# Attention output projection on float16 pairs, with Wo's rows pre-scaled on GpSimd and its squares taken in the down stage

## The chip, the cores and the metric

The kernel runs on one core of a Trainium2 chip. The metric is the device time of one execution in microseconds (us), smaller being better. A core has five engines that run their own instruction streams in order and wait for each other through semaphores: TensorE (PE for its matmuls, PEld for its weight loads), VectorE (DVE), ScalarE (ACT), GpSimd (POOL), and SyncE (SP), which here issues all DMAs from one queue.

## The reference

A layer norm of x (1024 x 512) feeds two branches, attention and a feed-forward branch with 4-bit weights. The result is x plus the attention output times a SiLU of the feed-forward output. Cut to what matters:

```python
xn = layernorm(x)
q, k = rmsnorm(xn @ Wq.T, q_norm_w), rmsnorm(xn @ Wk.T, k_norm_w)   # 32 query heads, 8 key heads
v = xn @ Wv.T                                                      # 8 value heads of 128
scores = q . k / sqrt(128) + alibi_slope * (key - query), causal
out = softmax(scores) @ v                                          # 32 heads of 128 -> 4096
s = out @ Wo.T                                                     # 4096 -> 512
g = silu(ffn(xn))                                                  # gate, up, down, group-dequantized
return x + s * g
```

## The kernel before, in words

The order of every engine's work is written out by hand. There are four stages.

**Gate and up, then down.** The two first feed-forward products run over 14 tiles of 128 hidden features. The down product then loops over the same 14 tiles (`it`, 0 to 13) and, in each, over two halves of the 1024 rows (`tb`). It works on float32r pairs: ACT copies a high part (`dnh`, `hh`, L102), DVE subtracts it to get the low part (`dnl`, `hl`, L104), and PE does three matmuls per product, high x high, high x low, low x high, in `mm3` (L108 to L110). The down weights are loaded as integers with their zeros and scales (`dn_load`, L409 to L414), dequantized by DVE (L419) and GpSimd (L420). The tiles with the tags `gs` and `us` hold gate and up sums and are free from about the fifth iteration on.

**Projections.** Twelve projections of 512 columns (four times keys and values of a pair of head groups, then two of queries) run over 8 row tiles each, on float16 pairs. `al`, the factor that scales each value column into float16's range, comes from the sums of squares of Wv; its reciprocal with the constants lands in `rv`, one factor per partition and group of heads (`undo`, L527).

**Attention.** 8 groups of heads, 4 query blocks of 256 rows each, 4 heads in a block: 128 units of 2 query tiles, so 256 steps. A block is 8 steps. In most groups the blocks come in the order 2, 3, 0, 1, and block 3 has the most keys, 896 and 1024. `step(n)` does, in this order, the scores of step n on PE, the exponentials of step n - 1 (DVE L816, ACT L817), the high half of the probabilities of n - 3 (ACT L827), the low half of n - 4 (DVE L836) with a DMA transpose of it on SP (L837), the product with the values of n - 9 on PE (`av`), and one group of three output-projection matmuls at n - 18. `pT` holds the transposed probabilities of four units. Scores have two PSUM buffers.

**Output projection.** When a unit's `av` is complete, ACT writes its high half `oh` times `rv` (L864) and DVE the low half `ol` (L870), both as float32r. Wo's 4096 x 512 rows come in 32 tiles of 128 x 512: `load_wo` (L775) on SP, `split_wo` with ACT's copy `woh` (L781) and GpSimd's subtraction `wol` (L782), both float32r. A tile's load comes 10 steps and its split 6 steps before the group's first use, four tiles at every second step, so that in the order above loads stand in steps 8 to 14 and splits in steps 12 to 18 of a group's 32 (block 3 is steps 8 to 15). The products of a group's four heads add up in PSUM (`op`); `accumulate` adds them on DVE to `y` (L905 copy for the first group, L907 add) and, for the last group, multiplies them by the gate (L910).

```python
        for lead, act in ((WO_SPLIT, split_wo), (WO_LOAD, load_wo)):
            w, r = divmod(m + lead, NB * BS)
            if 0 <= w < HKV and r in range(0, 2 * NH, 2):
                act(w, r // 2)
```

Of the kernel before, what the change touches and what calls it, by code (L numbers as in the profile page):

```python
# [10 lines left out]
F32 = mybir.dt.float32  # L11
F32R = mybir.dt.float32r
# [9 lines left out]
P = 128  # L22
# [30 lines left out]
VALUES_BLOCK = 3  # L53

WO_SPLIT = 6
WO_LOAD = 10

GATE_LOADS = [25, 26, 28, 30]
# [12 lines left out]
def attention_gated_by_ffn_kernel(ctx, tc, x, gu_w, gu_z, gu_s, dn_w, dn_z, dn_s, wq, wkv, wo, qnw, knw, out):  # L71
# [43 lines left out]
    ones_bf = const.tile([P, P], BF16, name="ones_bf")  # L115
    ve.memset(ones_bf, 1.0)
    rv = const.tile([P, HKV], F32, name="rv")
    wn = const.tile([P, HD], F32, name="wn")
    cs = const.tile([P, NH], F32, name="cs")
    rc = const.tile([P, 1], F32, name="rc")  # L120
# [309 lines left out]
    def dn_split_h(it, tb):  # L430
# [2 lines left out]
        split_r(h[:, it, tb * 512 : tb * 512 + 512], hh, hl)  # L433
        dn_h_hl[it, tb] = (hh, hl)


    qwb = wp.tile([P, HD], F32, name="qwb")
    kwb = wp.tile([P, HD], F32, name="kwb")
# [28 lines left out]
    class Projection:  # L467
# [55 lines left out]
        def undo(self):  # L523

            if self.kind == "kv":
                ve.reciprocal(self.ri, self.ri)
                ve.tensor_scalar(rv[:, 2 * self.i : 2 * self.i + 2], self.ri, 1.0 / (X_SCALE * P_SCALE), None, ALU.mult)  # L527

        def split_head(self, i):
            if i == 0:  # L530
# [157 lines left out]
    for it in range(NI):  # L688
        for tb in range(2):
            if it == 0:  # L690
                two = [pair(f"dn_ps{tb}_{i}") for i in range(2)]
                acc[tb] = [two[i // 2][:, i % 2, :] for i in range(4)]
            if tb == 0:
                if it + 2 < NI:
                    dn_dequant(it + 2)
                if it + 3 < NI:
                    dn_load(it + 3)
                if it + 1 < NI:
                    dn_split_w(it + 1)
            if it + 1 < NI:  # L700
                dn_split_h(it + 1, tb)
            wh, wl = dn_w_hl[it]
            hh, hl = dn_h_hl.pop((it, tb))
            for i in range(4):
                c = slice(i * P, i * P + P)
                mm3(acc[tb][i], (hh[:, c], hl[:, c]), (wh, wl), it == 0, it == NI - 1)
            if tb:
                if it in (1, 2):
                    gu_total((NI - 1, None), it - 1)
                elif it == 3:  # L710
                    gu_finish(0)
                elif it == 4:
                    gu_finish(1)
                elif it == 5:
                    norm_weights()
                elif NI - 6 <= it < NI - 1:
                    prepare(0, 8 - NI + it)
                if it == NI - 2:
                    prepare(1, -1)
            if it == NI - 1:  # L720
                for i in range(4):
                    go = h[:, i, tb * 512 : tb * 512 + 512]
                    se.activation(go, acc[tb][i], AF.Silu)
                    sp.dma_start(gd[tb * 4 + i], go)
# [42 lines left out]
    def load_queries(g, qb):  # L767
# [2 lines left out]
            qT[g, qb].rearrange("p t a g q -> p t (a g q)"), qd[g][qb * NQT : (qb + 1) * NQT].rearrange("t p c -> p t c")  # L770
        )

    def load_wo(g, i):
        wor[g, i] = late[0].tile([P, DM], F32, tag="wor", name=f"wor{g}_{i}", bufs=2)
        sp.dma_start(wor[g, i], wo[(g * NH + i) * HD : (g * NH + i + 1) * HD, :])  # L775

    def split_wo(g, i):
        woh[g, i] = late[0].tile([P, DM], F32R, tag="woh", name=f"woh{g}_{i}", bufs=5)
        wol[g, i] = late[0].tile([P, DM], F32R, tag="wol", name=f"wol{g}_{i}", bufs=5)
        raw = wor.pop((g, i))  # L780
        se.copy(woh[g, i], raw)  # L781
        ge.tensor_tensor(wol[g, i], raw, woh[g, i].bitcast(F32), ALU.subtract)  # L782

    def relative(g):

        rel = trel[g] = ap1.tile([P, S], F32, tag="trel", name=f"trel{g}")
        if g == 0:
            ge.iota(rel, pattern=[[-1, S]], base=S - P, channel_multiplier=1, allow_small_or_imprecise_dtypes=True)
            ge.affine_select(rel, rel, pattern=[[-1, S]], compare_op=ALU.is_ge, fill=1e20, base=S - P, channel_multiplier=1)
            ge.tensor_scalar(rel, rel, rc, float(SLOPES[NH - 1]), ALU.mult, ALU.mult)  # L790
        else:
            ge.tensor_scalar(rel, trel[g - 1], float(SLOPES[g * NH + NH - 1] / SLOPES[g * NH - 1]), None, ALU.mult)
# [65 lines left out]
            )  # L858

    def heads_hi(u):  # L860
        oh = late[0].tile([P, QB], F32R, tag="oh", name=f"oh{u}", bufs=8)
        ol = late[0].tile([P, QB], F32R, tag="ol", name=f"ol{u}", bufs=8)
        g = units[u][0]
        se.activation(oh, av_ps[u], AF.Copy, scale=rv[:, g : g + 1])  # L864
        oT[u] = (oh, ol)

    def heads_lo(u):
        oh, ol = oT[u]
        g = units[u][0]
        ve.scalar_tensor_tensor(ol, av_ps.pop(u), rv[:, g : g + 1], oh.bitcast(F32), ALU.mult, ALU.subtract)  # L870

    nb = len(units) // NH

# [25 lines left out]
    def accumulate(b, i):  # L899
        g, qb = blocks[b]  # L900
        ps = op_ps.pop((b, i))
        t = qb * NQT + i
        yt = y_[0][:, t, :]
        if g == 0:
            ve.tensor_copy(yt, ps)  # L905
        elif g < HKV - 1:
            ve.tensor_tensor(yt, yt, ps, ALU.add)  # L907
        else:
            gt = gates[b][:, 0, i]
            ve.tensor_tensor(gt, gt, ps, ALU.mult)  # L910
# [12 lines left out]
    def step(n):  # L923
        nonlocal last_ps
        if n < nn:
            u, qt = order[n]
            g, qb, hh = units[u]
            b = u // NH
            if qt == 0 and hh == 1 and b + 1 < nb:
                load_queries(*blocks[b + 1])  # L930
            if qt == 0 and hh == 3 and g + 1 < HKV:
                if b % NB == KEYS_BLOCK:
                    relative(g + 1)
                    load_keys(g + 1)
# [12 lines left out]
        b, r = divmod(n - AV_LAG - BS - 2, BS)  # L947
        if 0 <= b < nb - 1 and r % NH == NH - 1 and n < nn + AV_LAG + 1:
            accumulate(b, r // NH)
        finish_step()  # L950
        m = n - AV_LAG - BS - 1

        def project():
            b, r = divmod(m, BS)
            if 0 <= b < nb - 1:
                out_proj(b, *divmod(r, NH))

        if at(n - AV_LAG):
# [12 lines left out]
        b, r = divmod(n - AV_LAG, BS)  # L971
        if r == 2 and b in GATE_LOADS:
            gate_load(nb - NB + GATE_LOADS.index(b))
        if b in GATE_SUMS and 0 <= r - GATE_STEP < NQT:
            gate_partial(nb - NB + GATE_SUMS.index(b), r - GATE_STEP)
        for lead, act in ((WO_SPLIT, split_wo), (WO_LOAD, load_wo)):
            w, r = divmod(m + lead, NB * BS)
            if 0 <= w < HKV and r in range(0, 2 * NH, 2):
                act(w, r // 2)

    last_ps = None
    relative(0)
    early = 0
    for k, p in enumerate(projections):
        if k == len(projections) - 3:
            load_keys(0)
            load_values(0)
            load_queries(*blocks[0])
        for t in range(NT):
            prepare(k + 1, t)  # L990
            if t == NT - 2:
                prepare(k + 2, -1)
            if k + 2 < len(projections) and t < KT:
                projections[k + 2].load(t)
            if t == HT:
# [54 lines left out]
```

## Time and profile before

| | |
|---|---|
| median of 3 runs | 1081.96 us (1079.21 to 1083.37) |
| the profiled execution | 1087.19 us, span 1085.4 us, granted clock 0.987 |
| PE busy | 1025.6 us, 94% of the span |
| DVE busy | 885.4 us, 82% |
| ACT busy | 797.9 us, 74% |
| POOL busy | 362.7 us, 33% |
| DMA moved | 198.10 MB, mean 183 GB/s |
| stages, about | gate and up to 137 us, down to 217, projections to 500, attention to the end |

Busy time is the union of an engine's instructions; matmuls overlap, so their durations add up to more than it. "L108" is a line of the kernel. For a group of instructions the page gives busy us, the mean ns of one, then the engine's idle time before them and what ended it. The waits list who waited for whom, in all, how many times, and the longest.

### The profile page before, as it was taken

To read this page: it belongs to the slowest core of one execution; us is meant where nothing else is said; L and a number is where in the kernel's file an instruction comes from. 1 tells how busy PE (TensorE), PEld (TensorE's weight loads), DVE (VectorE), ACT (ScalarE), POOL (GpSimd) and SP (SyncE) were. 2 spreads that over 40 slices of the span, in tenths; PEclk is the share of its full clock that TensorE was granted. 3 is DMA by queue.
4 is the path that set the end of the run, shared out by engine and by line. 5 is a ranking of instruction groups with operands and counts; after the bars stand their busy time and mean duration, and the time that the engine had idled before them with its cause. 6 is when DMAs were issued, how large, how long until landed. Compare 5 with 4: busy or idle time off the path is not lost.

```text
span 1085.4 us, 18417 instructions
## 1 busy us (share of the span) xinstructions
PE 1025.6 (94%) x5912; PEld 621.8 (57%) x5912; DVE 885.4 (82%) x1738; ACT 797.9 (74%) x2144; POOL 362.7 (33%) x343
## 2 busy tenths in 40 slices
PE   7899899999999999997999999999899999999996
PEld 4444378744444444445667666667566676676674
DVE  7888997448777887787799897998897887979985
ACT  5777633568688776787788796887785887868872
POOL 1688653125545554341204104014031040043132
PEclk8999999999999999998999999999999999999999
DMA  5133255236989989999989999999998998999994
GB/s 198 32 114 119 67 141 155 74 124 152 237 206 202 237 196 270 223 205 203 221 170 213 190 216 193 196 201 189 206 191 178 213 201 184 193 224 220 237 192 117
DMA packets 445887, 198.10 MB, mean 183 GB/s; under 512 B 394402, under 2 KB 403934, under 8 KB 445790
## 3 DMA queue, kind: packets, MB, share of 16 engines
q1 hardware_dynamic: 445790, 196.93, 83.1%
q8 instruction: 46, 0.75, 0.3%
q14 instruction: 51, 0.42, 0.1%
HBM read 71.03 MB, written 29.36 MB: 92 GB/s over the span
## 4 chain that ended last, share of the span: by engine, by line
PE 57%; DVE 12%; ACT 11%; DMA 10%; issue 6%; POOL 2%; SPq 0%; DVEq 0%; ACTq 0%; POOLq 0%
DMA pT<-p 9%; PE gu_ps L255 6%; PE av L108 4%; PE s L108 4%; PE av L110 4%; PE av L109 4%; PE s L109 4%; PE s L110 4%; PE op L108 3%; PE op L110 3%; PE op L109 3%; ACT p L827 3%; PE ps_q L109 2%; PE ps_q L108 2%; PE ps_q L110 2%
## 5 line engine op out<-in xcount | busy, mean ns | idle before, releaser
L836 DVE SCALAR_TENSOR_TENSOR p<-pf,row,p 128x1024 f16<-128x1024 f32 (+7 forms) x256 | 216.4, 845 | 39.2 <-ACT p L827 36.3
L816 DVE CUSTOM_DVE_ANT_0 pf<-s,trel,cs 128x1024 f32<-128x1024 f32 (+7 forms) x256 | 207.5, 810 | 23.1 <-PE s L110 21.8
L817 ACT ACTIVATE pf<-pf,row 128x1024 f32<-128x1024 f32 (+7 forms) x256 | 197.0, 770 | 35.1 <-DVE row L816 33.5
L827 ACT ACTIVATE p<-pf,row 128x1024 f16<-128x1024 f32 (+7 forms) x256 | 196.9, 770 | 34.1 <-DMA pT<-p 30.1
L782 POOL TENSOR_TENSOR wol<-wor,woh 128x512 fp32r<-128x512 f32 x32 | 57.8, 1807 | 425.0 <-ACT woh L781 418.7
L108 PE MATMUL av<-pT,vT 128*128 128x256 f16 (+1 forms) x640 | 171.8, 268 | 25.6 <-DMA pT<-p 25.4
L109 PE MATMUL av<-pT,vT 128*128 128x256 f16 (+1 forms) x640 | 169.2, 264 | 0.0
L110 PE MATMUL av<-pT,vT 128*128 128x256 f16 (+1 forms) x640 | 169.2, 265 | 0.0
L108 PE MATMUL s<-kT,qT 128*128 128x512 f16 (+3 forms) x384 | 125.9, 328 | 3.8 <-DVE row L816 3.8
L109 PE MATMUL s<-kT,qT 128*128 128x512 f16 (+3 forms) x384 | 125.6, 327 | 0.0
L108 PEld LDWEIGHTS <-vT 128*128 128x128 f16 x640 | 62.5, 98 | 108.8 <-issue 84.6
L110 PE MATMUL s<-kT,qT 128*128 128x512 f16 (+3 forms) x384 | 123.8, 327 | 0.0
L108 PE MATMUL op<-woh,oh 128*128 128x512 f32 x248 | 121.9, 492 | 0.0
L864 ACT ACTIVATE oh<-av,rv 128x256 fp32r<-128x256 f32 x128 | 60.0, 468 | 57.5 <-PE av L110 56.3
L110 PE MATMUL op<-woh,ol 128*128 128x512 f32 x248 | 98.9, 399 | 0.0
L109 PE MATMUL ps_q<-wl_q,xth 128*128 128x512 f16 x256 | 97.7, 382 | 0.8 <-DVE wl_q L535 0.8
L108 PE MATMUL ps_q<-wh_q,xth 128*128 128x512 f16 x256 | 97.8, 382 | 0.6 <-ACT wh_q L534 0.6
L109 PE MATMUL op<-wol,oh 128*128 128x512 f32 x248 | 97.7, 394 | 0.0
L110 PE MATMUL ps_q<-wh_q,xtl 128*128 128x512 f16 x256 | 97.6, 381 | 0.0
L870 DVE SCALAR_TENSOR_TENSOR ol<-av,rv,oh 128x256 fp32r<-128x256 f32 x128 | 61.2, 478 | 21.8 <-ACT oh L864 21.7
L609 POOL TENSOR_TENSOR f_q<-f_q,inv_q 128x512 f32<-128x512 f32 x64 | 76.9, 1226 | 1.3
L109 PEld LDWEIGHTS <-vT 128*128 128x128 f16 x640 | 63.7, 99 | 11.9 <-issue 2.5
(184 smaller groups left out, 2263.5 us busy)
## 6 DMA issues: line engine op xcount, KB each, us to landing
qd<-tr_q SPq DMA_DIRECT2D x64, 256.0 KB, 3.5
qT<-qd SPq DMA_DIRECT2D x32, 512.0 KB, 4.4
wq<-in_wq SPq DMA_DIRECT2D x32, 256.0 KB, 4.1
wor<-in_wo SPq DMA_DIRECT2D x32, 256.0 KB, 3.6
gui<-in_gu_w SPq DMA_DIRECT2D x13, 512.0 KB, 3.6
wkv<-in_wkv SPq DMA_DIRECT2D x16, 256.0 KB, 3.8
vd<-v SPq DMA_DIRECT2D x8, 512.0 KB, 4.2
kd<-tr_kv SPq DMA_DIRECT2D x32, 128.0 KB, 2.5
```

The source lines that it names most:

```text
L108: te.matmul(ps, lhsT=lh, rhs=rh, start=first, stop=False)
L109: te.matmul(ps, lhsT=lh, rhs=rl, start=False, stop=False)
L110: te.matmul(ps, lhsT=ll, rhs=rh, start=False, stop=last)
L255: te.matmul(banks[j][:, k, :], lhsT=w[:, j, ws], rhs=x[:, j, k * 512 : k * 512 + 512], start=x is xth, stop=x is xtl)
L609: ge.tensor_tensor(f, f, ib, ALU.mult)
L782: ge.tensor_tensor(wol[g, i], raw, woh[g, i].bitcast(F32), ALU.subtract)
L816: ve.tensor_tensor_reduce(p, ps, trel[g][:, S - w :], cs[:, hh : hh + 1], 3e38, ALU.add, ALU.min, least[:, c])
L817: se.activation(p, p, AF.Exp, bias=least[:, c], scale=-1.0, accum_out=total[:, c])
L827: se.activation(p16[u, qt][:, :, 0, :], pf[u, qt], AF.Copy, scale=scale[:, qt : qt + 1])
L836: ve.scalar_tensor_tensor(lo, p, scale, hi, ALU.mult, ALU.subtract)
L864: se.activation(oh, av_ps[u], AF.Copy, scale=rv[:, g : g + 1])
L870: ve.scalar_tensor_tensor(ol, av_ps.pop(u), rv[:, g : g + 1], oh.bitcast(F32), ALU.mult, ALU.subtract)
```

## The change

Four things go together.

- Wo's pairs and the heads' pairs become float16. So that Wo's values lie in float16's range, each Wo row (a partition of its tile) is multiplied on GpSimd by the values' factor `rv` of its group times one factor `sg` per group of heads (`scale_wo`, lead 8: two steps after the load and two before the split). The heads are scaled by a constant only.
- The factor `sg` comes from the sum of squares of the group's Wo rows. Wo is loaded a second time, 1 MB per group, in the down stage at iterations 3 to 10 into the `gs` and `us` tiles; ACT squares it with an accumulator at iterations 5 to 12. `wo_factors` turns the sums into `sg`, its reciprocal `isg` and `rvs` = `rv` x `sg` at three points of the last key-value projection and the next one.
- `accumulate` multiplies each product by `isg` of its group.
- Wo's raw tiles get four buffers instead of two.

```diff
+WO_SCALE = 8
+    def wo_squares_load(g):
+        wo_raw[g] = gp.tile([P, NH, DM], F32, tag=("gs", "us")[g % 2], name=f"wo_sq{g}")
+        sp.dma_start(wo_raw[g], wo[g * NH * HD : (g + 1) * NH * HD, :].rearrange("(i p) c -> p i c", p=P))
+    def wo_squares(g):
+        w = wo_raw.pop(g).rearrange("p i c -> p (i c)")
+        se.activation(w, w, AF.Square, accum_out=swo[:, g : g + 1])
...
-                ve.tensor_scalar(rv[:, 2 * self.i : 2 * self.i + 2], self.ri, 1.0 / (X_SCALE * P_SCALE), None, ALU.mult)
+                ve.tensor_scalar(rv[:, 2 * self.i : 2 * self.i + 2], self.ri, 1.0 / X_SCALE, None, ALU.mult)
...
             if tb:
+                if 0 <= it - 3 < HKV:
+                    wo_squares_load(it - 3)
+                if 0 <= it - 5 < HKV:
+                    wo_squares(it - 5)
...
+    def wo_factors(k):
+        if k == 0:
+            ve.tensor_tensor(rvs, rv, rv, ALU.mult)
+            ve.tensor_tensor(swo16, rvs, swo, ALU.mult)
+        elif k == 1:
+            wo_ps.append(ps2("wo_ps")[:, 0, :HKV])
+            te.matmul(wo_ps[0], lhsT=ones_bf, rhs=swo16, start=True, stop=True)
+        else:
+            ve.tensor_scalar(sg, wo_ps.pop(), 1.0 / W_SCALE**2, 1e-30, ALU.mult, ALU.max)
+            rsqrt_seed(sg, sg)
+            ve.reciprocal(isg, sg)
+            ve.tensor_tensor(rvs, rv, sg, ALU.mult)
     def load_wo(g, i):
-        wor[g, i] = late[0].tile([P, DM], F32, tag="wor", name=f"wor{g}_{i}", bufs=2)
+        wor[g, i] = late[0].tile([P, DM], F32, tag="wor", name=f"wor{g}_{i}", bufs=4)
+    def scale_wo(g, i):
+        ge.tensor_scalar(wor[g, i], wor[g, i], rvs[:, g : g + 1], None, ALU.mult)
     def split_wo(g, i):
-        woh[g, i] = late[0].tile([P, DM], F32R, tag="woh", name=f"woh{g}_{i}", bufs=5)
-        wol[g, i] = late[0].tile([P, DM], F32R, tag="wol", name=f"wol{g}_{i}", bufs=5)
+        woh[g, i] = late[0].tile([P, DM], F16, tag="woh", name=f"woh{g}_{i}", bufs=5)
+        wol[g, i] = late[0].tile([P, DM], F16, tag="wol", name=f"wol{g}_{i}", bufs=5)
...
     def heads_hi(u):
-        se.activation(oh, av_ps[u], AF.Copy, scale=rv[:, g : g + 1])
+        se.activation(oh, av_ps[u], AF.Copy, scale=1.0 / P_SCALE)
     def heads_lo(u):
-        ve.scalar_tensor_tensor(ol, av_ps.pop(u), rv[:, g : g + 1], oh.bitcast(F32), ALU.mult, ALU.subtract)
+        ve.scalar_tensor_tensor(ol, av_ps.pop(u), 1.0 / P_SCALE, oh, ALU.mult, ALU.subtract)
...
+        undo = isg[:, g : g + 1]
         if g == 0:
-            ve.tensor_copy(yt, ps)
+            ve.tensor_scalar(yt, ps, undo, None, ALU.mult)
         elif g < HKV - 1:
-            ve.tensor_tensor(yt, yt, ps, ALU.add)
+            ve.scalar_tensor_tensor(yt, ps, undo, yt, ALU.mult, ALU.add)
         else:
-            ve.tensor_tensor(gt, gt, ps, ALU.mult)
+            ve.scalar_tensor_tensor(gt, ps, undo, gt, ALU.mult, ALU.mult)
...
-        for lead, act in ((WO_SPLIT, split_wo), (WO_LOAD, load_wo)):
+        for lead, act in ((WO_SPLIT, split_wo), (WO_SCALE, scale_wo), (WO_LOAD, load_wo)):
...
+    WO_FACTORS = [(last_kv, 5), (last_kv, 7), (last_kv + 1, 0)]
...
+            if (k, t) in WO_FACTORS:
+                wo_factors(WO_FACTORS.index((k, t)))
```

More of the change, by code (lines that the diff above doesn't have):

```diff
@@ L117, in attention_gated_by_ffn_kernel @@
     rv = const.tile([P, HKV], F32, name="rv")
+    swo = const.tile([P, HKV], F32, name="swo")
+    swo16 = const.tile([P, HKV], BF16, name="swo16")
+    sg = const.tile([P, HKV], F32, name="sg")
+    isg = const.tile([P, HKV], F32, name="isg")
+    rvs = const.tile([P, HKV], F32, name="rvs")
     wn = const.tile([P, HD], F32, name="wn")
@@ L434, in dn_split_h @@
         dn_h_hl[it, tb] = (hh, hl)
+    wo_raw = {}
+    def wo_squares_load(g):
[4 more added lines that the diff above has]
+        se.activation(w, w, AF.Square, accum_out=swo[:, g : g + 1])
     qwb = wp.tile([P, HD], F32, name="qwb")
@@ L771, in load_queries @@
         )
+    def wo_factors(k):
[10 more added lines that the diff above has]
+            ve.tensor_tensor(rvs, rv, sg, ALU.mult)
     def load_wo(g, i):
-        wor[g, i] = late[0].tile([P, DM], F32, tag="wor", name=f"wor{g}_{i}", bufs=2)
+        wor[g, i] = late[0].tile([P, DM], F32, tag="wor", name=f"wor{g}_{i}", bufs=4)
         sp.dma_start(wor[g, i], wo[(g * NH + i) * HD : (g * NH + i + 1) * HD, :])
+    def scale_wo(g, i):
+        ge.tensor_scalar(wor[g, i], wor[g, i], rvs[:, g : g + 1], None, ALU.mult)
     def split_wo(g, i):
-        woh[g, i] = late[0].tile([P, DM], F32R, tag="woh", name=f"woh{g}_{i}", bufs=5)
-        wol[g, i] = late[0].tile([P, DM], F32R, tag="wol", name=f"wol{g}_{i}", bufs=5)
+        woh[g, i] = late[0].tile([P, DM], F16, tag="woh", name=f"woh{g}_{i}", bufs=5)
+        wol[g, i] = late[0].tile([P, DM], F16, tag="wol", name=f"wol{g}_{i}", bufs=5)
         raw = wor.pop((g, i))
         se.copy(woh[g, i], raw)
-        ge.tensor_tensor(wol[g, i], raw, woh[g, i].bitcast(F32), ALU.subtract)
+        ge.tensor_tensor(wol[g, i], raw, woh[g, i], ALU.subtract)
     def relative(g):
@@ L860, in heads_hi @@
     def heads_hi(u):
-        oh = late[0].tile([P, QB], F32R, tag="oh", name=f"oh{u}", bufs=8)
-        ol = late[0].tile([P, QB], F32R, tag="ol", name=f"ol{u}", bufs=8)
-        g = units[u][0]
-        se.activation(oh, av_ps[u], AF.Copy, scale=rv[:, g : g + 1])
+        oh = late[0].tile([P, QB], F16, tag="oh", name=f"oh{u}", bufs=8)
+        ol = late[0].tile([P, QB], F16, tag="ol", name=f"ol{u}", bufs=8)
+        se.activation(oh, av_ps[u], AF.Copy, scale=1.0 / P_SCALE)
         oT[u] = (oh, ol)
@@ L868, in heads_lo @@
         oh, ol = oT[u]
-        g = units[u][0]
-        ve.scalar_tensor_tensor(ol, av_ps.pop(u), rv[:, g : g + 1], oh.bitcast(F32), ALU.mult, ALU.subtract)
+        ve.scalar_tensor_tensor(ol, av_ps.pop(u), 1.0 / P_SCALE, oh, ALU.mult, ALU.subtract)
     nb = len(units) // NH
@@ L979, in step @@
                 act(w, r // 2)
-    last_ps = None
+    last_ps, wo_ps = None, []
     relative(0)
+    last_kv = len(projections) - 3
+    WO_FACTORS = [(last_kv, 5), (last_kv, 7), (last_kv + 1, 0)]
     early = 0
```

## The prediction

> **What bounds the kernel now.** I read the page's busy shares first, then the same engines block by block inside attention, then the chain of waits there, then the starts of single matmuls, then SyncE's queue. TensorE is busy 94% of the span, VectorE 82%, and the DMA row is at 9 in nearly every slice of attention, so three resources are close together and shares alone decide nothing. The block table splits group 4 of the attention stage (a block is 8 steps: 4 heads x 2 query tiles; these four are query blocks 2, 3, 0, 1). Columns: stretch and its length, then busy us of PE, PEld, DVE, ACT, POOL, the granted clock, DMA share, GB/s.
>
> ```profile
> 763.80:782.70 18.90, 17.50 (x119) 11.32 (x118) 16.14 (x33) 15.30 (x33) 0.00 (x0) 1.00 1.09 216
> 782.70:805.00 22.30, 22.30 (x143) 14.21 (x142) 21.15 (x36) 19.58 (x35) 3.89 (x2) 1.00 1.00 203
> 805.00:826.80 21.80, 18.74 (x143) 14.07 (x142) 15.76 (x39) 13.87 (x38) 8.97 (x5) 0.95 1.01 174
> 826.80:840.60 13.80, 13.80 (x83) 9.03 (x81) 10.94 (x31) 10.11 (x29) 0.00 (x0) 0.96 0.75 176
> ```
>
> In the long block (second line) PE never idles, 22.30 of 22.30, with DVE 1.15 us behind; in the block after it PE loses 3.1 us. The waits say to what: the transposed probabilities. The first line is PE's only large wait in 520 to 1085 us, the second is SyncE held up by a Wo buffer.
>
> ```profile
> PE av L108 <- DMA pT<-p: 19.8, 19, 2.6
> ...
> SPq L775 <- POOL wol L782: 13.3, 11, 2.2
> ```
>
> The chain in the same 565 us puts the output projection (op) at 6.5 + 6.4 + 6.3 = 19.2%, 108 us:
>
> ```profile
> by line: DMA pT<-p 15.0%; PE av L108 7.7%; PE s L108 6.9%; PE s L109 6.9%; PE av L110 6.9%; PE av L109 6.8%; PE s L110 6.8%; PE op L108 6.5%; PE op L110 6.4%; PE op L109 6.3%; issue 4.8%; ACT p L827 3.7%; ACT pf L817 3.2%; DVE pf L816 2.2%;
> ```
>
> Matmuls overlap, so their recorded durations (394 ns for op, 379 for a float16 one) are no price. The price is start to start, in the timeline (start, duration):
>
> ```profile
> 801.06 0.27 PE L110 MATMUL av<-pT,vT 128*128 128x256 f16 x1
> ...
> 801.09 0.48 PE L108 MATMUL op<-woh,oh 128*128 128x512 f32 x1
> ...
> 801.40 0.39 PE L109 MATMUL op<-wol,oh 128*128 128x512 f32 x1
> ...
> 801.63 0.40 PE L110 MATMUL op<-woh,ol 128*128 128x512 f32 x1
> 801.87 0.10 PEld L108 LDWEIGHTS <-vT 128*128 128x128 f16 x1 [0.27 <-issue]
> 801.87 0.23 PE L108 MATMUL av<-pT,vT 128*128 128x128 f16 x1
> ...
> 802.05 0.38 PE L108 MATMUL s<-kT,qT 128*128 128x512 f16 x1
> ...
> 802.27 0.38 PE L109 MATMUL s<-kT,qT 128*128 128x512 f16 x1
> ...
> 802.48 0.38 PE L110 MATMUL s<-kT,qT 128*128 128x512 f16 x1
> ```
>
> From the av matmul before a group of three op matmuls to the av matmul after it: 0.81 us. Over all 248 groups the median steps are 28, 315, 231 and 239 ns, 813 in all, and the av matmul after starts its successor 10 ns late (its weights could not be loaded ahead: the 0.27 "issue"). Float16 matmuls of the same shape follow each other after 216 ns, a 256-column av after 109: 109 + 3 x 216 = 757. A group can save 813 + 10 - 757 = **66 ns**.
>
> **What the Trainium skill says.** "TensorE: Matmul & The Clock Gate", section Back-to-back issue gap, gives N/2.4 + 2.5 ns, 216 for 512 columns; the float16 starts above agree. Its section on weight-path modes says the fast weight load is off for FP32; the trace agrees: 190 ns for op's loads, 98 for float16. "SBUF — State Buffer", section SBUF: two separate sides, says GpSimd and a VectorE instruction with two SBUF inputs take one port pair as an exclusive lock, the later one waiting. The trace agrees for tensor-tensor work: L836 at 809.94, started just after GpSimd's L609, took 1.93 us where 1.15 is usual at that width; and L782, started at 802.81 under an L836 that ended at 803.37, ended 1.14 us after it. L816, L870 and L907 read PSUM and one SBUF tensor and show no such loss.
>
> **The change part by part**, against the profiled execution's own 1087.19 us (span 1085.4). The median of the runs is 1081.96, 5.2 less; I carry the difference over to it.
>
> (1) Float16 pairs in op. 256 groups x 66 ns = 16.9 us of PE time. On the chain are 108 of the op groups' 256 x 704 ns = 180 us, 60%. So **-10.1**; ends: -16.9 if everything follows PE, 0 if DVE or the transposes are next at once. What is late next is DVE in the long blocks (21.15 of about 21.8) and the transposes after them.
>
> (2) Wo's buffers go from 2 to 4. L775 then finds its buffer free a whole group earlier, and SP's 13.3 us of waiting goes. Behind it in SP's queue stand the transposes of the long block: at 796.4 SP waits until 798.64 though the next L836 had ended at 797.5, so about 1.1 of 2.2 us is real delay, and it is upstream of the 3.1 us that PE loses in the next block. Per group I take 0.3 us at the end: **-2** (0 to -7; above 0 is excluded, a wait goes and nothing is queued instead).
>
> (3) GpSimd scales 32 tiles of Wo (scale_wo). No row shows this form at this size. From below, the pass over the position table at L789 with a pointer scalar took 1152 ns for 1024 columns, so about 0.7; from above, half of L792's 2970, 1.5. Together 22 to 48 us on an engine that is busy at most 9 us of a 20 us block: itself hidden. Its queue is where it can hurt: 3 of 4 scalings of a group fall into the long block, where DVE has 1.15 us to spare. A scaling follows the subtraction L782, which ends some 1.1 us after an L836; the next L836 starts 1.3 to 2 us after the last. Overlap about 0.2 us, 32 times = 6 us of DVE, a quarter on the chain: **+1.5** (0 to +17). L782 with a float16 input and output: 1.14 us assumed as now (0.9 to 1.8), hidden: the product needs its tile three steps later. ACT's copy now waits for the scaling. From load to copy are four steps, 8 us and more, against 3.6 landing + 1.5, so nothing, except in group 0: its first load is issued at 497.8 and copied at 501.9, where ACT would be late by about 1 us, and its exponentials behind that: **+0.7**.
>
> (4) Accumulation gains a factor: L907 (680 ns) and L905 (683) become forms like L204 at 512 columns (742). 56 x 62 ns + 8 at the end = 4 us of DVE over 32 blocks, 0.12 a block, against 1.15 to spare: **+0.8** (0 to +4). L864 and L870 lose a pointer and write float16; v's casts at L567 and L568 (402 and 421 ns) suggest nothing dearer than 468 and 478: 0.
>
> (5) Squares in the down stage. Each is 2048 columns on ACT: L490 takes 1052 for 1024, L485 633 for 512, slope 0.82, so 1.9 + 0.19 for the accumulator = 2.1 us, eight times 17. ACT waits 39.8 us there for PE, in two gaps an iteration (5.44 us), and with 1.85 of copies, 2.1 of squares and 0.8 of head splits it has 4.8. Only at the end, where square 7 meets projection 1's four squares (3.5 us), do the Silus come late: **+0.6** (0 to +3). DMA: 8 x 1 MB = 4096 packets at 84 to 108 ns on 16 engines, 22 to 28 us, into a stage with a share of 0.44 of 80 us. SP issues eight more; behind them stand dn_z and dn_s, needed two iterations (10.9 us) later and landing after 3.7 + 3.5. Hidden; if that cover goes, PE waits for the difference (0 to +8).
>
> (6) wo_factors: seven small DVE instructions of about 0.2 us, one tiny matmul, ordered behind a tile of 2.6 us each: **+0.2** (0 to +2).
>
> Sum: -10.1 - 2 + 1.5 + 0.7 + 0.8 + 0.6 + 0.2 = **-8.3**: profiled about 1078.9, median **1073.7**.
>
> **Rivals.** A: PE's gain is handed to the next wait. For: DVE at 95% in the long blocks, a DMA share of 1.0, 15% of the chain in transposes. Against: the (2) relief works at exactly that place, and blocks such as 826.80 have DVE at 79%. Then (1) shrinks to -3 and the sum to about -1: 1081. B, slower: GpSimd's scalings lock DVE out. Place: L836 in the long block, three scalings of up to 1.0 us blocked each, 3 us on top of 21.15 + 0.12, giving 24.3 instead of 22.3: +2 in each of 7 blocks = +14, while the other blocks still save about 6: +8 to profile, 1090. It decides from where a scaling blocks DVE by 0.7 us. For: the 0.78 us lost at 809.94. Against: L792, the nearest form, runs beside L836 with little loss, and a one-input form holds the port for a shorter time. That the product isn't faster at all (separate weight loads for 768 matmuls) is spoken against by the score matmuls, which have them and keep 216 ns.
>
> **How the numbers follow.** A measurement of this kernel tells about 0.5%, 5.4 us, from no change. Forecast 0.63 (its own range 1064 to 1076), A 0.22, B and what else makes it slower (a late down stage) 0.15. The range 1063 to 1086 goes from the forecast with most of (1) and (2) realised to B half paid.
>
> **What would show it.** Right: op starts 216 ns apart, no "issue" after the group, op's chain share near 17%, long blocks of 21.8 us, no SP wait on a wol, smaller PE waits for pT. Wrong: L836 longer than before in the long blocks (B), PE's wait for pT grown by 10 us (A), dn_ps waiting for hl or dnh (5).

## The result, and the profile after

| | before | after |
|---|---|---|
| median of 6 runs each, same chip | 1082.66 us (1079.21 to 1086.24) | 1075.24 us (1069.99 to 1077.16) |
| ratio of the two, 95% interval | | 0.9921 [0.9897, 0.9945] |
| the profiled execution | 1087.19 us, span 1085.4 us | 1077.16 us, span 1075.4 us |
| granted clock over the span | 0.987 | 0.983 |

The changed kernel is 0.8% faster, 8.5 us by the ratio. Its line numbers move on: the matmuls of `mm3` are L109 to L111, the exponentials L854 and L855, the halves of the probabilities L865 and L874, Wo's load L810, its scaling L813, its split L819 and L820, the heads' halves L901 and L906.

The starts of matmuls on PE around one output-projection group (start, duration), as in the prediction's last fence:

```profile
797.64 0.27 PE L111 MATMUL av<-pT,vT 128*128 128x256 f16 x1
797.75 0.38 PE L109 MATMUL op<-woh,oh 128*128 128x512 f16 x1
797.96 0.38 PE L110 MATMUL op<-wol,oh 128*128 128x512 f16 x1
798.18 0.38 PE L111 MATMUL op<-woh,ol 128*128 128x512 f16 x1
798.39 0.22 PE L109 MATMUL av<-pT,vT 128*128 128x128 f16 x1
```

From the av matmul ahead of the group to the one behind it are now 0.75 us, against the 757 ns that were worked out and 813 before; over all groups of this form the median is 757 ns. The starts are about 0.215 us apart and no "issue" follows the group.

The block table of group 4, query blocks 2, 3, 0, 1 (stretch and length, busy PE, PEld, DVE, ACT, POOL, granted clock, DMA share, GB/s):

```profile
761.00:779.70 18.70, 16.94 (x120) 10.37 (x118) 16.52 (x36) 15.20 (x33) 0.00 (x0) 1.00 1.10 218
779.70:801.50 21.80, 21.80 (x144) 13.29 (x142) 21.09 (x36) 19.33 (x35) 7.27 (x5) 1.00 1.12 218
801.50:819.40 17.90, 16.93 (x143) 12.69 (x141) 15.68 (x40) 13.65 (x38) 11.27 (x7) 1.00 0.98 194
819.40:834.20 14.80, 12.89 (x83) 7.37 (x82) 11.73 (x33) 10.10 (x29) 0.00 (x0) 1.00 0.75 168
```

The long block (second line) is 21.80 us instead of 22.30, and PE is still busy in all of it. The block behind it fell from 21.80 to 17.90 us, at full clock instead of 0.95. That is the largest fall of any group: over the six blocks that stand right behind a long one the sum went from 117.1 to 111.9 us. Of the other two blocks of this group one is 0.2 us shorter and one 1.0 us longer (18.70 against 18.90, 14.80 against 13.80): PE idles 1.8 and 1.9 us in them now.

The chain of waits in attention, 520 us to the end, by line, and then the largest wait of PE in the same stretch and SyncE's wait over the whole span (total, times, longest, us):

```profile
by line: DMA pT<-p 13.8%; issue 8.4%; PE av L109 6.6%; PE s L109 6.5%; PE s L111 6.5%; PE s L110 6.5%; PE av L111 6.2%; PE av L110 6.2%; PE op L111 5.8%; PE op L110 5.8%; PE op L109 5.7%; ACT pf L855 4.5%; ACT p L865 4.2%; DVE pf L854 3.5%;
```

```profile
PE av L109 <- DMA pT<-p: 21.3, 18, 2.3
```

```profile
SPq L810 <- POOL wol L820: 1.8, 2, 1.1
```

The output projection has 5.8 + 5.8 + 5.7 = 17.3% of the chain instead of 19.2%, SyncE's wait for a `wol` fell from 13.9 to 1.8 us over the whole span (another 2.3 us are waits for a scaling, L813). PE's wait for transposed probabilities is as long as it was (21.3 against 19.8 us), so this one of the forecast's signs did not come. "issue" and the exponentials took up part of the chain that op left. From the page, the new GpSimd operation (busy us, mean ns, then the idle time before it), and the two kinds of Wo loads by size and median time to landing:

```profile
L813 POOL TENSOR_SCALAR wor<-wor,rvs 128x512 f32<-128x512 f32 x32 | 53.0, 1656 | 313.0 <-DMA wor<-in_wo 313.0
...
wo_sq<-in_wo SPq DMA_DIRECT2D x8, 1024.0 KB, 9.0
wor<-in_wo SPq DMA_DIRECT2D x32, 256.0 KB, 3.6
```

A scaling takes 1.66 us in the mean, above the upper end of 1.5 that was assumed, and a 1 MB load of Wo lands after 9.0 us.

### The profile page after: what moved, and what is told of

Its sections match the earlier page's. It is cut to its first block, busy times and chain, and to the rows that moved or that the text cites. A ratio compares the mean times of both kernels' runs of the same rounds, so it can differ in the third digit from the quotient of the medians.

```text
span 1075.4 us, 18459 instructions
## 1 busy us (share of the span) xinstructions
PE 1012.7 (94%) x5913; PEld 588.1 (55%) x5913; DVE 884.4 (82%) x1745; ACT 803.0 (75%) x2160; POOL 409.0 (38%) x375
## 4 chain that ended last, share of the span: by engine, by line
PE 50%; DVE 13%; ACT 13%; DMA 12%; issue 8%; POOL 2%; SPq 1%; DVEq 0%; ACTq 0%; POOLq 0%
DMA pT<-p 7%; PE gu_ps L262 6%; PE av L109 3%; PE s L109 3%; PE s L111 3%; PE s L110 3%; PE av L111 3%; PE av L110 3%; PE op L111 3%; PE op L110 3%; PE op L109 3%; ACT pf L855 3%; ACT p L865 3%; DVE pf L854 2%; PE ps_q L109 2%
## 5 line engine op out<-in xcount | busy, mean ns | idle before, releaser
L874 DVE SCALAR_TENSOR_TENSOR p<-pf,row,p 128x1024 f16<-128x1024 f32 (+7 forms) x256 | 221.1, 864 | 36.1 <-ACT p L865 33.4
L855 ACT ACTIVATE pf<-pf,row 128x1024 f32<-128x1024 f32 (+7 forms) x256 | 197.3, 771 | 46.7 <-DVE row L854 44.2
L854 DVE CUSTOM_DVE_ANT_0 pf<-s,trel,cs 128x1024 f32<-128x1024 f32 (+7 forms) x256 | 207.3, 810 | 16.7 <-PE s L111 15.5
L865 ACT ACTIVATE p<-pf,row 128x1024 f16<-128x1024 f32 (+7 forms) x256 | 196.7, 769 | 29.5 <-DMA pT<-p 25.3
L109 PE MATMUL av<-pT,vT 128*128 128x256 f16 (+1 forms) x640 | 169.4, 265 | 26.3 <-DMA pT<-p 26.1
L813 POOL TENSOR_SCALAR wor<-wor,rvs 128x512 f32<-128x512 f32 x32 | 53.0, 1656 | 313.0 <-DMA wor<-in_wo 313.0
L111 PE MATMUL av<-pT,vT 128*128 128x256 f16 (+1 forms) x640 | 169.2, 265 | 0.0
L109 PE MATMUL s<-kT,qT 128*128 128x512 f16 (+3 forms) x384 | 126.1, 328 | 4.2 <-DVE row L854 4.1
L111 PE MATMUL s<-kT,qT 128*128 128x512 f16 (+3 forms) x384 | 124.6, 328 | 0.0
L109 PEld LDWEIGHTS <-vT 128*128 128x128 f16 x640 | 63.2, 99 | 71.5 <-issue 17.3
L109 PE MATMUL ps_q<-wh_q,xth 128*128 128x512 f16 x256 | 97.8, 382 | 0.3 <-ACT wh_q L551 0.3
L111 PE MATMUL ps_q<-wh_q,xtl 128*128 128x512 f16 x256 | 97.5, 381 | 0.0
L110 PE MATMUL op<-wol,oh 128*128 128x512 f16 x248 | 94.5, 381 | 1.0 <-POOL wol L820 1.0
L111 PE MATMUL op<-woh,ol 128*128 128x512 f16 x248 | 94.7, 382 | 0.0
L109 PE MATMUL op<-woh,oh 128*128 128x512 f16 x248 | 94.4, 381 | 0.0
L901 ACT ACTIVATE oh<-av 128x256 f16<-128x256 f32 x128 | 47.9, 374 | 42.8 <-PE av L111 41.6
L820 POOL TENSOR_TENSOR wol<-wor,woh 128x512 f16<-128x512 f32 x32 | 50.2, 1570 | 66.4 <-ACT woh L819 66.4
```

The source lines that it names most:

```text
L109: te.matmul(ps, lhsT=lh, rhs=rh, start=first, stop=False)
L110: te.matmul(ps, lhsT=lh, rhs=rl, start=False, stop=False)
L111: te.matmul(ps, lhsT=ll, rhs=rh, start=False, stop=last)
L813: ge.tensor_scalar(wor[g, i], wor[g, i], rvs[:, g : g + 1], None, ALU.mult)
L820: ge.tensor_tensor(wol[g, i], raw, woh[g, i], ALU.subtract)
L854: ve.tensor_tensor_reduce(p, ps, trel[g][:, S - w :], cs[:, hh : hh + 1], 3e38, ALU.add, ALU.min, least[:, c])
```

## The experiments

Theory: the faster product and the freed Wo buffers carry the gain, and the rest of the change costs little. Rivals: the product's saving is handed on to the next wait; GpSimd's scalings lock DVE out; the factors at the start of attention and the squares in the down stage cost what they delay. Each ratio is to runs of the kernel before on the same chip, with its 95% interval. A single profiled span varies by several us from run to run (the changed kernel's two profiles have 1075.4 and 1066.5), so sums over one trace show where time sits, and the medians say how much.

### Float16 by itself (e1), with four buffers (e2), and two buffers in the changed kernel (e3)

e1 is the kernel before with four tiles in float16 and nothing else:

```diff
-        woh[g, i] = late[0].tile([P, DM], F32R, tag="woh", name=f"woh{g}_{i}", bufs=5)
+        woh[g, i] = late[0].tile([P, DM], F16, tag="woh", name=f"woh{g}_{i}", bufs=5)
...
-        ol = late[0].tile([P, QB], F32R, tag="ol", name=f"ol{u}", bufs=8)
+        ol = late[0].tile([P, QB], F16, tag="ol", name=f"ol{u}", bufs=8)
```

(`wol` and `oh` likewise.) e2 adds `bufs=4` for `wor`. e3 is the changed kernel with `bufs=2` for `wor`.

> The kernel before with only the four tiles woh, wol, oh and ol in float16: no scaling of Wo, no squares, no factor in the accumulation, two Wo buffers. It leaves out the scaling that keeps Wo's low parts in float16's normal range. Theory 1 (the gain is the 66 ns a group that TensorE saves, where op is on the chain): 8 to 12 us under the kernel before, about 1072, with op starts 216 ns apart. Theory 2 (TensorE's saving is handed to the waits for the transposes; the gain came from the buffers and from cheaper evictions): at most 3 us under it, and the waits of av for pT grow from about 20 us by 5 or more. For the evictions: if oh and ol become 374 and 418 ns here, it is the output type; if they stay at 468 and 478, it was the constant in place of the pointer.

> As the float16-only kernel, with four buffers for Wo's raw tiles instead of two. Theory 1: SP's 13 us of waiting for wol go, and the end moves by 0 to 3 us more. Theory 2: by 5 us or more beyond the float16-only kernel.

> The changed kernel with two Wo buffers again. Theory 1: 0 to 3 us slower than the changed kernel (1075 to 1078). Theory 2: 5 us or more slower (1080 and up), with SP waiting for wol 13 us or more again.

Measured: e1 1075.25 us, 0.9942 [0.9922, 0.9962]; e2 1068.42 us, 0.9887 [0.9850, 0.9925]; e3 1074.93 us, 0.9939 [0.9920, 0.9958].

So float16 by itself gives 0.58%, 6.3 us, not the 10.1 of step (1). I added up the lengths of the blocks of each query block, from the third block on (8 blocks each of 1 and 0, 7 each of 2 and 3; 66 ns times 8 groups a block is 4.2 us for eight blocks and 3.7 for seven):

| sum of block lengths, us | block 2 | block 3 (long) | block 0 (mostly behind it) | block 1 |
|---|---|---|---|---|
| before | 125.8 | 155.9 | 162.1 | 122.1 |
| e1, float16, 2 buffers | 125.7 | 152.3 | 158.3 | 121.9 |
| e2, float16, 4 buffers | 122.7 | 152.3 | 152.0 | 122.5 |
| after | 125.2 | 152.2 | 155.7 | 120.7 |

Two traces of one kernel differ by up to 4 us in a row of block 0 (the changed kernel's second trace, e9, has 151.9) and by up to 1.4 in the others. Float16 pays in full in the long block (-3.6 us), where all traces of one type agree to 0.3 us. In block 0 the sum fell by 3.8 and in blocks 2 and 1 not at all. But the 66 ns did arrive there too. Over all these blocks, PE's time without idle time and without what half clock adds (half of every stretch in which the granted clock is half) fell by 15.5 us from before to e1. What ate about half of it is PE's idle time, 3.3 us more, and spells of half clock, 4.4 us more. Block 2 of group 7 shows both, first before, then in e1:

```profile
985.30:1004.40 19.10, 17.31 (x119) 11.31 (x117) 18.33 (x37) 16.48 (x37) 5.66 (x4) 1.00 1.17 240
```

```profile
973.20:994.80 21.60, 18.44 (x120) 10.91 (x118) 17.92 (x38) 16.45 (x37) 5.06 (x4) 0.92 1.11 202
```

PE waits 3.16 us for transposed probabilities in the second one, and in the 5 us after it the clock is 0.70 in the mean. A wait does not always bring this: e2 has one of 3.00 us at 518.09 with full clock behind it. From e4 to e3, the same step in the changed kernel, idle time grew by 7.6 us and the loss to half clock by 3.4.

So faster matmuls made PE wait more. Its wait for transposed probabilities from 520 us on is 19.8 us before and 16.9 in e4, but 23.4 in e1 and 25.7 in e3, with float16 and two buffers. With four it is 17 to 21 us again (17.2 in e9, 19.1 in e2, 21.3 in the changed kernel).

What bounds the block behind the long one is seen in e1 and e2, in group 4, where they differ most. The block table of e1, block 0, and SyncE's wait in e1:

```profile
796.30:817.40 21.10, 18.30 (x143) 13.02 (x142) 15.61 (x41) 13.97 (x38) 8.73 (x5) 0.95 1.00 186
```

```profile
SPq L775 <- POOL wol L782: 10.3, 9, 2.0
```

The long block and block 0 in e2:

```profile
774.00:795.80 21.80, 21.80 (x144) 13.29 (x142) 21.11 (x36) 19.57 (x35) 3.70 (x2) 1.00 1.08 219
795.80:813.90 18.10, 16.82 (x143) 12.58 (x141) 15.54 (x41) 14.09 (x38) 8.74 (x5) 1.00 1.05 187
```

The same 143 matmuls take 18.10 us instead of 21.10. With four buffers SyncE's wait for `wol` is gone from the list of e2 (1.1 us are left in e10), PE idles 1.3 us instead of 2.8 and it keeps its full clock (1.00 against 0.95). That transposes are no longer held back behind the waiting load is the reading of this; it fits all traces: the six blocks right behind a long one take 117.1 us before, 114.0 (e1) and 114.3 (e3) with float16 and two buffers, and 107.6 to 112.6 in the eight traces with four buffers and the loads in their old place. The medians put the buffers at 0.55% (e1 to e2), about 6 us, or 0.40% (e1 to e10), about 4, with float16 and no scaling. In the changed kernel (e3 to after) the step is 0.9939 to 0.9921, about 2 us, which the intervals don't resolve. No run has four buffers without float16.

### The changed kernel on float32r with two buffers (e4)

The four tiles back to float32r, `wor` back to two buffers; the factors, scalings, squares and `accumulate` stay.

```diff
-        woh[g, i] = late[0].tile([P, DM], F16, tag="woh", name=f"woh{g}_{i}", bufs=5)
+        woh[g, i] = late[0].tile([P, DM], F32R, tag="woh", name=f"woh{g}_{i}", bufs=5)
...
-        wor[g, i] = late[0].tile([P, DM], F32, tag="wor", name=f"wor{g}_{i}", bufs=4)
+        wor[g, i] = late[0].tile([P, DM], F32, tag="wor", name=f"wor{g}_{i}", bufs=2)
```

> The changed kernel with the four tiles in float32r and two Wo buffers (four don't fit with float32r). Everything else of the change stays: scaling, squares, factors. Theory 1: 8 to 12 us slower than the changed kernel with two buffers, so 1084 to 1089, slower than the kernel before by the price of the added work. Theory 2: within 3 us of the changed kernel with two buffers. Evictions: oh 374 and ol 418 ns if the constant in place of the pointer made them cheaper, 468 and 478 if the type did.

Measured: 1080.50 us, 0.9994 [0.9982, 1.0007]. Everything in the change but float16 and buffers adds up to nothing that can be told from none: -0.6 us, between -1.9 and +0.8. And e4 to e3, float16 alone once more, is 0.55%, 5.9 us: the second estimate of step (1). The SyncE wait is there again:

```profile
SPq L810 <- POOL wol L820: 12.9, 11, 2.3
```

A term on the other side, which the prediction had put at nothing, shows in the evictions of the heads. From the pages' groups, first e1 (pointer scalar `rv`, float16 out), then e4 (constant scalar, float32r out); the number after the bar is busy us, then mean ns:

```profile
L864 ACT ACTIVATE oh<-av,rv 128x256 f16<-128x256 f32 x128 | 59.5, 465 | 44.7 <-PE av L110 43.6
L870 DVE SCALAR_TENSOR_TENSOR ol<-av,rv,oh 128x256 f16<-128x256 f32 x128 | 61.2, 478 | 20.5 <-ACT oh L864 20.3
```

```profile
L901 ACT ACTIVATE oh<-av 128x256 fp32r<-128x256 f32 x128 | 48.3, 377 | 54.9 <-PE av L111 54.5
L906 DVE SCALAR_TENSOR_TENSOR ol<-av,oh 128x256 fp32r<-128x256 f32 x128 | 53.5, 418 | 23.1 <-ACT oh L901 22.8
```

The type makes no difference (468 before and 465 in e1 on ACT, 478 in both on DVE); the constant in the pointer's place does: 465 - 377 = 88 ns on ACT and 60 ns on DVE, 11 and 8 us over 128 units. In busy time, that outweighs the accumulation's factor (743 ns at L944, as the 742 that were worked out, +4 us of DVE) on the same engine.

### Later factors (e5), no squares (e6), no scaling (e7)

All three are the changed kernel with one edit. e5 moves the three parts of `wo_factors` later; e6 takes the squares' loads and instructions out and sets their sums to a constant; e7 leaves the scaling out.

```diff
-    WO_FACTORS = [(last_kv, 5), (last_kv, 7), (last_kv + 1, 0)]
+    WO_FACTORS = [(last_kv, 5), (last_kv + 1, 5), (last_kv + 2, 3)]
```

```diff
+    ve.memset(swo, 4 * DM * 0.0147**2)
...
-                if 0 <= it - 3 < HKV:
-                    wo_squares_load(it - 3)
-                if 0 <= it - 5 < HKV:
-                    wo_squares(it - 5)
```

```diff
-        for lead, act in ((WO_SPLIT, split_wo), (WO_SCALE, scale_wo), (WO_LOAD, load_wo)):
+        for lead, act in ((WO_SPLIT, split_wo), (WO_LOAD, load_wo)):
```

> The changed kernel with the last two points of wo_factors later: the matmul one projection later, at tile 5, and what follows at tile 3 of the last one. If PE's wait of 2.6 us for the sums in front of wo_ps and the half clock behind it are what puts the first scores of attention at 441.8 us instead of 434.3, the first scores come back to 433 to 435 us, and the end is 2 to 4 us earlier. Rival: the steps that run early have slack, as they had caught up all but 1.8 us by block 2, and the end moves by at most 1.8 us.

> The changed kernel without the second load of Wo and without its squares; the sums are set to a constant near their value, the rest is the same. If the down stage's cost is DVE waiting 4.0 us for kwb's DMA behind 1 MB loads, the 1.5 us that the eighth down iteration loses and that DVE wait are gone, and the end is 1 to 2 us earlier. If ACT's 17 us or the DMA load cost more than that (later weights for the projections), 3 us or more.

> The changed kernel without the 32 scalings on GpSimd: Wo goes unscaled into the product, so the output lacks the values' factor and the group's. If the port lock matters as priced, L874 falls from 864 to about 845 ns (5 us of DVE in all) and the end is 1 to 2 us earlier. If a scaling stands in the way of ACT's copy or of the long blocks' DVE by more, 4 us or more.

Measured: e5 1073.94 us, 0.9935 [0.9917, 0.9953]; e6 1068.75 us, 0.9899 [0.9851, 0.9946]; e7 1068.66 us, 0.9883 [0.9854, 0.9912]. Against the changed kernel's 0.9921, e5 is not faster, and e6 and e7 are lower by 0.2% and 0.4%, 2 to 4 us each, with intervals that overlap. Beside e4, where all of these parts together cost -1.9 to +0.8 us, both can be right in full only if the cheaper evictions, which are in that sum, earn as much.

**The factors.** PE's starts in the changed kernel where the tiny matmul stands in the projections (in brackets: idle before, and the releaser), and the following 5 us in the block table:

```profile
434.86 0.17 PE L801 MATMUL wo_ps<-swo,ones_bf 128*128 128x8 bf16 x1 [2.56 <-DVE swo L798]
...
435.15 0.63 PE L110 MATMUL ps_kv<-wl_kv,xth 128*128 128x512 f16 x1
435.58 0.63 PE L111 MATMUL ps_kv<-wh_kv,xtl 128*128 128x512 f16 x1
436.00 0.63 PE L109 MATMUL ps_kv<-wh_kv,xth 128*128 128x512 f16 x1
```

```profile
435.00:440.00 5.00, 5.00 (x17) 1.86 (x15) 1.39 (x4) 3.96 (x15) 3.14 (x8) 0.66 1.47 311
```

DVE runs over two tiles behind PE there, so PE waits 2.56 us for the factors' sum, and afterwards it runs at a granted clock of 0.66: starts 0.43 us apart, twice the usual 0.216. Attention's first scores came 7.5 us later than before (441.8 against 434.3), 1.3 us of which had been lost before the projections began. But by the third block only 1.8 us were left (515.3 against 513.5; 512.7 in e9). The kernel before has a wait of its own at this place, 3 us after its first scores, with a granted clock of 0.69 from 437 to 442:

```profile
PE n_ps L496 <- ACT sb_q L488: 2.0, 1, 2.0
```

The changed kernel doesn't have it: the wait for the factors' sum stands in its place. The last projection starts 3.5 us later than before (465.1 against 461.6). Without the 1.3 us that is 2.2 us for the factors; in e9, counted in the same way, 1.3. e5 put the wait elsewhere, and the other one came back:

```profile
PE wo_ps L801 <- DVE row L854: 5.4, 1, 5.4
PE n_ps L513 <- ACT sb_q L505: 2.4, 2, 2.2
```

The first scores come at 435.2, the last projection is 8.7 us late instead, and the third block starts at 515.9. The end doesn't move. That the first scores' delay goes through to the end found no support; but as e5 moves a wait and doesn't remove it, what the factors cost at the end isn't measured.

**The squares.** Who waited for whom in the down stage (137 to 217 us) of the changed kernel:

```profile
DVE wn L461 <- DMA kwb<-in_knw: 4.0, 1, 4.0
...
PE dn_ps L111 <- DVE hl L105: 2.2, 3, 1.2
```

The norm weights' tile `kwb` (the second of two small loads at `it` = 5, L460) stands behind the 1 MB loads in SyncE's queue. DVE waits 4.0 us for it at L461, the low half `hl` behind it is late, and the iteration `it` = 7 takes PE 6.91 us instead of 5.44. Without the squares (e6) there is no wait for `kwb`, and the iteration takes 5.44 us again. The squares' own instructions take 2.1 us (1912 ns and 183 for the accumulator), as worked out, and neither they nor the Silus are what is late.

**The scaling.** The sum of the long blocks is 152.3 us in e2, 152.2 in the changed kernel and in e3, so three scalings per long block cost nothing there. L874 in the 1024-wide form did become longer than before (1317 ns), but not through the scalings: it is as long without them. First the changed kernel, then e7:

```profile
L874 DVE SCALAR_TENSOR_TENSOR p<-pf,row,p 128x1024 f16<-128x1024 f32 x32 | 45.3, 1416 | 5.6 <-ACT p L865 5.4
```

```profile
L874 DVE SCALAR_TENSOR_TENSOR p<-pf,row,p 128x1024 f16<-128x1024 f32 x32 | 45.6, 1425 | 5.3 <-ACT p L865 5.2
```

And e4, which has the scalings, stands at 1292. The 896-wide form is 1253 ns with the scalings and 1182 without. Over all forms the mean is 864 against 855 ns (863 to 871 in the other float16 traces with scalings in this place), so 2 to 4 us of DVE in all, about 0.1 us for each of the 32 scalings. Whether scaling costs anything at the end, no run here shows.

### Late factors and early norm weights (e8)

e5's edit, and the two loads of the norm weights moved to iteration 1 of the down stage, ahead of the squares' loads:

```diff
     def norm_weights():
-        sp.dma_start(qwb, qnw.partition_broadcast(P))
-        sp.dma_start(kwb, knw.partition_broadcast(P))
...
+                if it == 1:
+                    norm_loads()
```

> The changed kernel with the late factors and with the loads of the two norm weights four iterations ahead of their use in the down stage, before the Wo loads begin. Expected: the late factors' gain plus up to 1.5 us in the down stage; together 3 to 5 us under the changed kernel, about 1071. Rival: under 2 us, where both losses were taken up by slack later.

Measured: 1073.84 us, 0.9927 [0.9896, 0.9957]. The wait for `kwb` is gone, and the 1.5 us of PE with it; the end shows no gain that can be told from none.

### The changed kernel again (e9), e2 again (e10), and Wo's loads in a lighter block (e11, e12)

e9 and e10 repeat two kernels without an edit, on one chip. In e11 (changed kernel) and e12 (e2) the Wo tiles of all groups but the first are loaded 26 steps ahead, and in e11 scaled 24 ahead, so that loads don't fall into the long block:

```diff
-        for lead, act in ((WO_SPLIT, split_wo), (WO_LOAD, load_wo)):
-            w, r = divmod(m + lead, NB * BS)
...
+        for first, later, act in ((WO_SPLIT, WO_SPLIT, split_wo), (WO_LOAD, 26, load_wo)):
+            for lead in {first, later}:
+                w, r = divmod(m + lead, NB * BS)
```

> The changed kernel once more, on the chip of the next three, so that the difference to the float16-only kernel with four buffers is measured directly. If scaling, squares and factors cost what the runs so far suggest, 1074 to 1076, 5 to 7 us above that kernel; if those were differences between chips, within 2 us of it.

> The float16-only kernel with four Wo buffers once more, beside the changed kernel (no scaling, so Wo's low parts lie below float16's normal range): 1067 to 1070 if the first runs told right.

> The changed kernel with Wo's loads 26 and the scalings 24 steps ahead of their use from the second group on, so that both stand in the lightest block (query block 1) of the group before; splits stay. If the scalings cost by locking VectorE out in the long blocks, L874 falls to about 850 ns and the end is 2 to 4 us earlier than the changed kernel. If they cost by their place in GpSimd's or ACT's queue around the splits, the same. If what costs is that GpSimd works at all, no change.

> The float16-only kernel with four Wo buffers and the loads 26 steps ahead, in the lightest block of the group before. If Wo's 1 MB a group competes with the transposes of the long blocks for the DMA engines, PE's waits for pT fall by 3 us or more and the end is 2 to 4 us under the float16-only kernel with four buffers; if the loads are hidden where they are, within 1.5 us.

Measured: e9 1072.32 us, 0.9919 [0.9892, 0.9946]; e10 1069.38 us, 0.9902 [0.9879, 0.9924]; e11 1081.96 us, 1.0008 [0.9993, 1.0024]; e12 1077.62 us, 0.9970 [0.9959, 0.9980].

e9 repeats the result. e10 stands 0.17% below it, 1.8 us, which the intervals don't resolve: whether scaling, squares and factors together cost anything stays open. e11 and e12 did not do what was expected of them: they are 10 and 8 us slower than e9 and e10. The block table of e12 for blocks 0, 1 of group 4 and block 2 of group 5, and the same two last blocks in e2:

```profile
801.40:818.30 16.90, 16.87 (x144) 12.73 (x143) 14.95 (x41) 13.89 (x38) 8.75 (x5) 1.00 0.97 190
818.30:835.30 17.00, 13.31 (x84) 7.42 (x82) 12.35 (x34) 10.91 (x31) 0.00 (x0) 0.94 0.83 185
835.30:854.30 19.00, 19.00 (x119) 11.33 (x118) 16.10 (x33) 14.95 (x33) 0.00 (x0) 0.87 1.11 228
```

```profile
813.90:828.40 14.50, 12.88 (x83) 7.37 (x82) 11.71 (x33) 10.35 (x29) 0.00 (x0) 1.00 0.80 173
828.40:847.40 19.00, 16.92 (x119) 10.25 (x118) 15.90 (x33) 15.31 (x33) 0.00 (x0) 1.00 1.10 214
```

Block 0 does become shorter (16.90 us, with PE busy in all of it), but block 1, into which the loads now fall, takes 17.00 us instead of 14.50, and PE's clock falls. From the third block on, blocks 1 and 2 take 126.4 and 130.1 us (e10: 123.9 and 123.9), and PE's wait for transposed probabilities rises from 19.1 us in e2 to 24.2 (longest 3.6 instead of 2.2). So the place of Wo's loads matters, and of the two that were tried the long block is the cheaper. That the loads meet there the transposes that PE needs soon, in the DMA engines or in SyncE's queue, is a reading of the two tables; it wasn't isolated.

The lowest times are those of float16 with four buffers (e2, e10): 0.9887 and 0.9902. That kernel leaves out the scaling that keeps Wo's low parts in float16's normal range, and it is not shown to beat the changed kernel.

## Why the prediction was right, and where its terms were off

The sum of -8.3 us met the measured -8.5, and the forecast's direction and its first cause, the faster op groups, hold. Its second cause, the freed buffers, shows in the traces and, without the scaling, in the medians. That the size met so well is in part luck, because errors in the steps cancel. Taken apart, float16 gives -5.9 us (e4 to e3), the two further buffers about -2 (e3 to after) and the rest -0.6 (e4), and of these only the first is clear of noise. By the prediction's steps:

**(1) The product, -10.1: price right, share at the end too large.** The 66 ns a group are there, but e1 and e4 to e3 give 6.3 and 5.9 us, 35 to 37% of 16.9 instead of 60%. What failed is taking op's share of the chain for the share of the saving that reaches the end. The chain tells where PE was last, not what it waits for once it is faster: PE idled more, mostly for transposed probabilities, and lost more to half clock after such waits. This came in all kinds of blocks but the long one, where PE never idles.

**(2) The buffers, -2: right in place, size between 2 and 6.** The block that was named became shorter, in all eight traces with four buffers. e1 to e2 gives 6 us, e1 to e10 about 4, and in the changed kernel about 2, unresolved. The 0 to -7 of the range holds all of them. What the step didn't count is the clock: block 0 of group 4 ran at 0.95 before and at 1.00 after. The expected smaller waits for transposed probabilities came only against float16 with two buffers, not against the kernel before.

**(3) Scaling, +1.5 and +0.7: duration above its bounds, effect not found.** L813 takes 1.66 us, not 0.7 to 1.5. The upper bound, half of L792, was near (1.49); the lower one was no guide (its 1152 ns belong to L790, not to L789, which is another operation). The overlap, put at 6 us of DVE, is 2 to 4, and the long block kept its 21.8 us. Rival B, which needed 0.7 us a scaling, is refuted, though not by its argument from L792: beside L792 one 384-wide row of L836 took 1258 ns, where 615 is usual. B's sign, longer rows of L836's kind in the long block, did come in the 1024-wide form, but e7 shows that the scalings were not the cause; what was stays open. In the first group ACT waited 6.3 us in three waits for scaled tiles, more than the 1 us foreseen, yet PE's wait for transposes between 495 and 525 us was no longer than before (5.0 against 5.6 us), so nothing shows of the +0.7.

**(4) Accumulation, +0.8: price right (743 for 742 ns), but the evictions beside it were not worth 0.** They became 94 ns cheaper on ACT and 60 on DVE. 12 us of ACT and 8 us of DVE in attention stand against the 4 us of accumulation. The prediction had compared them with casts from the projections and taken "nothing dearer" for "nothing". e4's total of about zero, where the steps (3) to (6) had +3.8, is consistent with that; how much of it the evictions earn was not measured by itself.

**(5) Squares, +0.6: size near, cause wrong.** PE lost about 1.5 us, not to late Silus but to `kwb`, a load behind the squares' loads in the queue; with `kwb` loaded earlier (e8) the loss is gone. The prediction had looked at dn_z and dn_s behind them and missed the two small loads with a near due time.

**(6) Factors, +0.2: local price too low, effect at the end not found.** "Ordered behind a tile of 2.6 us" was true of DVE; that PE reaches the matmul ahead of DVE and waits was not seen. It cost a 2.6 us wait in the first trace and 4.0 in e9. Since it stands in the place of a wait that the kernel before had, 1 to 2 us of it are left at the last projection.

Rival A was right in part: of the 7 us that it would have taken from step (1), about 4 did go. It didn't decide, because the buffers' relief came on top and the other steps added up to nothing (e4).

## What to carry to other kernels

Price a faster instruction by start-to-start times, and then ask block by block what its engine will wait for once it gets there earlier. Here the saving arrived in full only where PE never idles; elsewhere more than half of it came back as idle time and as spells of half clock after waits. Look at what a queue holds back before the block in which PE idles: two more buffers of 2 KB a partition gave 2 to 6 us. And where a large load is put into a queue, look for the small load behind it with the nearest due time. Before a delay is priced by the first thing it makes late, see whether another wait at the same place falls away.

## What the runs showed of the hardware

- A constant in place of a pointer scalar made an eviction from PSUM of 128x256 cheaper, whatever the output type: 465 to 374 ns on ACT (float16) and 468 to 377 (float32r), 478 to 418 on DVE for both.
- After a wait of 2.56 us PE's matmul starts were 0.43 us apart, twice the usual, for more than 3 us, at a granted clock of 0.66 over 5 us. Single waits for transposed probabilities went the same way in some cases and not in others: 0.70 over the next 5 us after 3.16 us (e1), 0.50 after 3.64 us (e12), but 1.00 after 3.00 us (e2). What decides it is not shown.
- GpSimd's scaling of a 128x512 float32 tile by a pointer scalar, in place, took 1.66 us, longer than the 1152 ns of the pass over 1024 columns at L790 in the kernel before. L792 there, over the same 1024 columns with a constant, took 2970.
